# Two-layer mixer, projection and mixture-of-experts kernel: the first batch's mixers in two halves of the tokens

## The chip, the cores and the metric

The kernel runs on one core of a Trainium2 chip. The metric is the device time of one execution, in microseconds; times given here are the median of three executions, or one profiled execution where a profile is read. PE is TensorE (matrix multiply), DVE is VectorE, ACT is ScalarE, POOL is GpSimd, SP is SyncE, which here only issues transfers. ACT and POOL issue transfers too, from the same in-order instruction queue as their other work.

## The reference, cut to what matters

Four batches of 1024 tokens with 1024 channels each. Layer 0 mixes the tokens and projects; layer 1 mixes them with other constants and goes through a routed mixture of experts with a shared expert.

```
def mixer(r, k, w, u, cond):              # k is also v; time t runs over 1024 tokens, per channel
    tf    = sigmoid(sum(cond))            # one number per batch
    decay = exp(-exp(w)) * (0.5 + 0.5 * tf)
    ek, ekv = exp(min(k, 30)), exp(min(k, 30)) * k
    forward  sums:  a_t = a_(t-1) * decay + x_t      for x in (ek, ekv)
    backward sums:  the same from the last token to the first
    euk = exp(min(u + k, 30))
    num = forward(ekv) + backward(ekv) - ekv + euk * k
    den = forward(ek)  + backward(ek)  - ek  + euk
    return sigmoid(r) * num / max(den, 1e-8) * (0.8 + 0.2 * tf)

x = x + mixer(x, f, w0, u0, cond) @ (weight * scale).T + bias          # layer 0
h = mixer(x, f, w1, u1, cond)                                          # layer 1
x = x + h' + routed_experts(rmsnorm(h')) + shared_expert(rmsnorm(h'))  # h' = what the gate makes of h
```

The backward sum needs the tokens after a given one, the forward sum those before it. Both layers take the same `f` for k and v; sigmoid(r) of layer 1 depends on layer 0's result, so the kernel applies it later ("the gate").

## The kernel before, in words

**Mixers.** Channels lie on the 128 partitions, tokens on the free axis. A *unit* is one batch, one tile of 128 channels (`ct`, eight of them) and one layer (`L`), so there are 16 units per batch. For batch 0 all eight layer-0 units come first, then the eight of layer 1, each with its own load of k; for later batches the two layers of one `ct` follow each other and share k, `ek` and `ekv`. `mixing()` is a generator that runs a software pipeline: its iteration s does, in this order,

- "forth": the two forward scans of unit s (L281, DVE) into `fg`, and on ACT their scaling (L284) and the start values `tail` of the backward scans (L282);
- "back": `euk` of unit s-1 (L291, ACT) and its two backward scans in place (L293, DVE);
- "begin": min and exp of the next unit's k (L253 on DVE, L254 on ACT), where the next unit has a k of its own;
- "quotient" of unit s-2: four DVE passes in layer 0 (L311 to L315), three in layer 1 (L317);
- "times": `ekv` of the next unit (L259);
- "sums" of unit s-1: two DVE passes (L324, L325), a transfer from POOL that adds `euk` to `num` (L326), and the reciprocal on ACT by Relu, Ln, Exp (L329 to L331);
- transfers from ACT's queue: x for the sigmoid (L335, layer 0), the next k (L248), and the store of unit s-2's result to `c0_d` or `c1_d` (L341). Only then is unit s-2 in `made`.

ACT has one function table at a time: `exp_ln` and `other` keep track of it, and a sigmoid between exponentials costs a table load each way.

**Matrix work.** A chunk `q` is 512 tokens, so a batch has two. `first_ffn(q)` is layer 0's projection (eight *pieces* of 16 matmuls, L433), `late_gate(q)` the gate of chunks whose layer-1 mixer was not ready at that time, `norm_route(q)` norm and routing, `shared_up(q)` and `shared_down(q)` the shared expert (L645, L673). The experts follow in a last stage that this change does not touch.

**Order.** Every engine's instructions are in the order in which the program emits them. `order()` writes the order of pieces out by hand; `run` emits mixer steps ahead of each piece as long as `work["vector"] < pace[0] * work["tensor"]`, two sums of estimated costs (`W_SCANS` and the like, 6.9 for a piece). `pace` is 1.0 at first and 0.9 from the first `shared_up` on. `mix_until(units)` emits, at once, whatever steps are missing until the named units are `made`:

```
410  def early(ot):
...
416      if ot == 0:
417          mix_until(*((b, ct, 0) for ct in range(NC)))
...
422              nc.sync.dma_start(out=c0s[ct], in_=c0_d[b, ct, :, cols])
```

`early` of a piece is called two pieces ahead. So a `first_ffn` waits for all eight layer-0 units of its batch, and what is emitted after that call stands behind those steps in each queue. In batches after the first, the eighth layer-0 unit is the fifteenth of sixteen units.

Of the kernel before, what the change touches and what calls it, by code (L numbers as in the profile page):

```python
# [8 lines left out]
FP = mybir.dt.float32  # L9
I32 = mybir.dt.int32  # L10
U32 = mybir.dt.uint32
AF = mybir.ActivationFunctionType
ALU = mybir.AluOpType
# [9 lines left out]
P = 128  # L23
# [8 lines left out]
def kernel(  # L32
# [176 lines left out]

    W_SCANS, W_MIN, W_PASS, W_HALF = 4.7, 0.7, 1.25, 0.75  # L210
    W_PIECE, W_SMALL = 6.9, 1.0
    LATENCY = 12.0
    PACE = 0.9
    table = [None]

    def exp_ln(to, of, func, **kw):
# [5 lines left out]
    def other(to, of, func, **kw):  # L222
        table[0] = func
        nc.scalar.activation(to, of, func, **kw)

    units = [(0, ct, L) for L in range(2) for ct in range(NC)]
    units += [(b, ct, L) for b in range(1, B) for ct in range(NC) for L in range(2)]
    group = []  # L230
    for s, (b, ct, L) in enumerate(units):
        group.append(group[-1] if b > 0 and L == 1 else s - sum(1 for u in units[:s] if u[0] > 0 and u[2] == 1))
    made = set()

    def mixing():


        n = len(units)
        firsts = {}
        for s in range(n):  # L240
            firsts.setdefault(group[s], s)
        ks, of = {}, {}

        def fetch(g):
            if g in firsts:
                b, ct, _ = units[firsts[g]]
                ks[g] = pk.tile([P, T], FP, name="k")
                nc.scalar.dma_start(out=ks[g], in_=fT[b, bass.ts(ct, P), :])  # L248

        def begin(g):  # L250

            ek = p1.tile([P, T], FP, name="ek")
            nc.vector.tensor_scalar(ek, ks[g], 30.0, None, ALU.min)  # L253
            exp_ln(ek, ek, AF.Exp)  # L254
            return ek

        def times(ek, g):
            ekv = p1.tile([P, T], FP, name="ekv")
            nc.vector.tensor_tensor(ekv, ek, ks[g], ALU.mult)  # L259
            return ekv  # L260

        fetch(0)
        fetch(1)
        ek = begin(0)
        ekv = times(ek, 0)
        xg = None
        for s in range(n + 2):
            new, last, old = ((u if 0 <= u < n else None) for u in (s, s - 1, s - 2))
            if old is not None and units[old][2] == 0:
                other(xg, xg, AF.Sigmoid)  # L270
            if new is not None:

                b, ct, L = units[new]
                dk = decay[L][:, ct, b : b + 1]
                fg = pfg.tile([P, 2, T], FP, name="fg")
                tail = pfg.tile([P, 2], FP, name="tail")
                of[new] = fg, tail
                for m, x in enumerate((ek, ekv)):  # L280
                    nc.vector.tensor_tensor_scan(fg[:, m, :], dk.to_broadcast([P, T]), x, 0.0, ALU.mult, ALU.add)  # L281
                nc.scalar.activation(tail, fg[:, :, T - 1], AF.Copy, scale=dk)  # L282
                flat = fg.rearrange("p a t -> p (a t)")
                nc.scalar.activation(flat, flat, AF.Copy, scale=rest[L][:, ct, b : b + 1])  # L284
                yield W_SCANS
            if last is not None:
                b, ct, L = units[last]
                fg, tail = of[last]

                euk = p1.tile([P, T], FP, name="euk")  # L290
                exp_ln(euk, ks[group[last]], AF.Exp, bias=v[f"u{L}"][:, ct : ct + 1])  # L291
                for m in range(2):
                    nc.vector.tensor_tensor_scan(  # L293
                        fg[:, m, ::-1],
                        decay[L][:, ct, b : b + 1].to_broadcast([P, T]),
                        fg[:, m, ::-1],
                        tail[:, m : m + 1],
                        ALU.mult,
                        ALU.add,
                    )  # L300
                yield W_SCANS
            begun = s + 1 < n and group[s + 1] != group[s]
            if begun:
                ek = begin(group[s + 1])
                yield W_MIN
            if old is not None:
                b, ct, L = units[old]
                den, num = of[old][0][:, 0, :], of[old][0][:, 1, :]

                done = r  # L310
                nc.vector.scalar_tensor_tensor(den, den, 1e-8, r, ALU.max, ALU.mult)  # L311
                nc.vector.scalar_tensor_tensor(done, den, 2.0, r, ALU.subtract, ALU.mult)
                if L == 0:
                    nc.vector.scalar_tensor_tensor(done, done, nosc[:, b : b + 1], num, ALU.mult, ALU.mult)
                    nc.vector.tensor_tensor(done, done, xg, ALU.mult)  # L315
                else:
                    nc.vector.tensor_tensor(done, done, num, ALU.mult)  # L317
                yield W_PASS * (4 - L)
            if begun:
                ekv = times(ek, group[s + 1])  # L320
                yield W_PASS
            if last is not None:
                den, num = of[last][0][:, 0, :], of[last][0][:, 1, :]
                nc.vector.scalar_tensor_tensor(den, euk, E30, den, ALU.min, ALU.add)  # L324
                nc.vector.scalar_tensor_tensor(euk, euk, E30, ks[group[last]], ALU.min, ALU.mult)  # L325
                nc.gpsimd.dma_start(out=num, in_=euk, accum_op=ALU.add)  # L326

                r = p2.tile([P, T], FP, name="r")
                nc.scalar.activation(r, den, AF.Relu, bias=ntiny)  # L329
                exp_ln(r, r, AF.Ln, bias=tiny)  # L330
                exp_ln(r, r, AF.Exp, scale=-1.0)  # L331
                if units[last][2] == 0:
                    b, ct, _ = units[last]
                    xg = pxg.tile([P, T], FP, name="xg")
                    nc.scalar.dma_start(out=xg, in_=xT[b, bass.ts(ct, P), :])  # L335
                yield 2 * W_PASS
            if begun:
                fetch(group[s + 1] + 1)
            if old is not None:
                b, ct, L = units[old]  # L340
                nc.scalar.dma_start(out=(c0_d, c1_d)[L][b, ct], in_=done)  # L341
                of.pop(old)
                made.add(units[old])

# [59 lines left out]
    def first_ffn(q, gated):  # L404
# [4 lines left out]
        def early(ot):  # L409
            if not gated:  # L410

                nc.sync.dma_start(out=resT_d[ot, :, bass.ts(q, CH)], in_=xT[b, bass.ts(ot, P), cols])
            else:
                xs[ot] = px.tile([P, CH], FP, name="x")
                nc.sync.dma_start(out=xs[ot], in_=xT[b, bass.ts(ot, P), cols])
            if ot == 0:
                mix_until(*((b, ct, 0) for ct in range(NC)))
                if q == 0:
                    work["tensor"] += LATENCY
                for ct in range(NC):  # L420
                    c0s.append(pc0.tile([P, CH], FP, name="c0"))
                    nc.sync.dma_start(out=c0s[ct], in_=c0_d[b, ct, :, cols])
            tiles[ot] = pw0.tile([P, NC, P], FP, name="w0t")
            nc.sync.dma_start(out=tiles[ot], in_=w0[ot])
            if gated:
                mix_until((b, ot, 1))
                c1s[q, ot] = (ph, pc1)[q % NCH].tile([P, CH], FP, name="c1")
                nc.sync.dma_start(out=c1s[q, ot], in_=c1_d[b, ot, :, cols])

# [20 lines left out]
    def gate(q, ot, x, lag=1):  # L450
# [7 lines left out]
            other(held["y"], x, AF.Sigmoid, bias=v["b0"][:, ot : ot + 1])  # L458


        each = q == 0
        if ot == 0:
            accs[q] = pacc.tile([P, CH], FP, name="acc")
        square = accs[q] if ot == 0 and not each else None
# [29 lines left out]
    def late_gate(q):  # L494
# [3 lines left out]
        xs = {}  # L498

        def load(ot):  # L500
            mix_until((b, ot, 1))
            c1s[q, ot] = (ph, pc1)[q % NCH].tile([P, CH], FP, name="c1")
            nc.sync.dma_start(out=c1s[q, ot], in_=c1_d[b, ot, :, cols])
            xs[ot] = px.tile([P, CH], FP, name="x")
            nc.sync.dma_start(out=xs[ot], in_=resT_d[ot, :, bass.ts(q, CH)])
# [388 lines left out]

    def order():

        pieces = first_ffn(0, False) + first_ffn(1, False) + late_gate(0)

        pieces.insert(-1, Piece(lambda: None, tensor=LATENCY / 3))
        pieces += [Piece(lambda: None, tensor=0.5) for _ in range(7)]  # L900

        def slower():
            pace[0] = PACE
            work["tensor"] = max(work["tensor"], work["vector"] / PACE)

        pieces.append(Piece(slower, tensor=0.0))
        up, gates = shared_up(0), late_gate(1)
        for i, piece in enumerate(up):
            pieces.append(piece)
            if i % 2 == 1:  # L910
                pieces.append(gates.pop(0))
        pieces += gates
        pieces += shared_down(0) + shared_up(1) + shared_down(1)
        pieces += first_ffn(2, True) + first_ffn(3, True) + shared_up(2) + shared_down(2) + shared_up(3)
        for b in range(2, B):
            q = NCH * b
            pieces += first_ffn(q, True) + first_ffn(q + 1, True) + shared_down(q - 1)
# [476 lines left out]
```

## Time and profile before

| what | value |
|---|---|
| median of three executions | 5108.35 us (5101.46 to 5109.7) |
| profiled execution | 5109.81 us, span 5107.8 us |
| busy: PE, DVE, ACT, POOL | 94%, 61%, 28%, 16% of the span |
| first matmul of `first_ffn(0)` | 197.09 us |
| first matmul of `shared_up(0)` | 370.61 us |
| first matmul of `first_ffn(2)` | 728.57 us |
| one forward scan of 1024 tokens | 2.28 us |
| one table load on ACT | 1.283 us |

Times count from the start of the span. The stages that matter are four: the layer-0 mixers of batch 0 with PE idle, the first two projections, the gate and routing of the first chunk with PE mostly idle, and from `shared_up(0)` to `first_ffn(2)` a stretch in which PE is busy and DVE works off batch 1's mixers. After `first_ffn(2)` the same pattern repeats by batch with a full PE.

### The profile page before, as it was taken

The numbers are of one execution on the slowest core, as the hardware profiler recorded it, in microseconds if no ns is written. First come the engines' busy times: TensorE is split into PE (matmuls) and PEld (weight loads), VectorE is DVE, ScalarE is ACT, GpSimd is POOL, SyncE is SP. The second block draws the span as 40 slices with busy tenths as digits, with TensorE's granted clock in tenths as the row PEclk, the third lists the DMA queues.
The fourth block names the chain that finished last, engine by engine and source line by source line (L and its number), as shares of the span: only waits on it lengthen the run. The fifth ranks groups of instructions, "written<-read, shape, count | busy, mean of one in ns | idle before, by whom it ended". The sixth has DMA issues, their size and how long they took to land.

```text
span 5107.8 us, 36503 instructions
## 1 busy us (share of the span) xinstructions
PE 4823.9 (94%) x12906; PEld 2235.0 (44%) x12906; DVE 3130.7 (61%) x3280; ACT 1445.5 (28%) x1840; POOL 818.4 (16%) x765
## 2 busy tenths in 40 slices
PE   0479999999999998999999999999999999999999
PEld 0124444444444443444444444444444444444444
DVE  9988887887860222656565656556565656565621
ACT  5557656566540210111111111111111111111110
POOL 0113202302310220111111111111111111111110
PEclk9989999999999999999999999999999999999999
DMA  4678679669754845676767676767676777777784
GB/s 139 192 206 216 181 222 269 174 198 277 194 160 127 236 128 189 214 233 220 233 216 241 212 241 212 241 214 239 214 239 214 239 229 224 229 224 229 224 233 118
DMA packets 524212, 1077.77 MB, mean 211 GB/s; under 512 B 30642, under 2 KB 260147, under 8 KB 523411
## 3 DMA queue, kind: packets, MB, share of 16 engines
q1 hardware_dynamic: 386338, 744.70, 42.9%
q0 software_dynamic: 74656, 223.12, 20.9%
q10 hardware_dynamic: 63024, 107.50, 6.0%
q8 instruction: 105, 1.72, 0.1%
q14 instruction: 89, 0.72, 0.0%
HBM read 844.13 MB, written 203.56 MB: 205 GB/s over the span
## 4 chain that ended last, share of the span: by engine, by line
PE 60%; ACT 0%; issue 0%; DVE 0%; ACTq 0%
PE gA L1117 14%; PE gC L1117 9%; PE gB L1117 9%; PE dA L1117 7%; PE dB L1117 5%; PE dC L1117 5%; PE tr L971 2%; PE gA L1005 2%; PE gB L1005 2%; PE tr L1054 1%; PE dA L1067 1%; PE dB L1067 1%; PE gB L1305 0%; PE gC L1305 0%; PE gA L1305 0%; PE dA L1305 0%
## 5 line engine op out<-in xcount | busy, mean ns | idle before, releaser
L645 PE MATMUL mm<-c,wpc 128*128 128x512 f32 x1792 | 777.7, 593 | 0.9 <-DMA wpc<-in_su 0.9
L433 PE MATMUL mm<-c,w0t 128*128 128x512 f32 x1024 | 447.9, 599 | 213.9 <-DMA w0t<-in_w 212.4
L645 PEld LDWEIGHTS mm<-c,wpc 128*128 128x128 f32 x1792 | 337.9, 190 | 416.1 <-issue 412.5
L1117 PE MATMUL gA<-w,hsT 128*128 128x512 f32 x1088 | 489.6, 593 | 0.0
L1117 PE MATMUL gC<-w,s_up 128*128 128x512 f32 x1088 | 489.1, 592 | 0.0
L1117 PE MATMUL gB<-t_up,s_up 128*128 128x512 f32 x1088 | 489.1, 592 | 0.0
L1101 POOL DMA_INDIRECT sum_d<-y,tokens x148 | 306.3, 2070 | 917.2 <-DMA sum_d<-y,tokens 541.8
L871 POOL DMA_INDIRECT hs<-h_d,tokens x146 | 147.7, 1012 | 1621.8 <-PE tr L971 1540.3
L433 PEld LDWEIGHTS mm<-c,w0t 128*128 128x128 f32 x1024 | 196.2, 192 | 461.8 <-issue 456.4
L673 PE MATMUL mm<-sact,wpc 128*128 128x512 f32 x896 | 395.2, 596 | 0.0
L1117 PEld LDWEIGHTS gB<-t_up,s_up 128*128 128x128 f32 x1088 | 206.7, 190 | 260.2 <-issue 244.2
L1117 PEld LDWEIGHTS gC<-w,s_up 128*128 128x128 f32 x1088 | 206.7, 190 | 260.2 <-issue 260.2
L838 DVE TENSOR_TENSOR t_up<-w,w 128x2048 f32<-128x2048 f32 x136 | 310.7, 2285 | 0.0
L1117 PEld LDWEIGHTS gA<-w,hsT 128*128 128x128 f32 x1088 | 201.7, 190 | 227.8 <-issue 227.8
L293 DVE TENSOR_TENSOR_SCAN fg<-decay,tail,fg 128x1024 f32<-128x1024 f32 x128 | 292.9, 2330 | 0.0
L1117 PE MATMUL dB<-t_down,s_down 128*128 128x512 f32 x544 | 256.9, 595 | 0.1
L1117 PE MATMUL dA<-w,actT 128*128 128x512 f32 x544 | 255.8, 592 | 0.0
L1117 PE MATMUL dC<-w,s_down 128*128 128x512 f32 x544 | 255.8, 592 | 0.0
L972 ACT COPY hsT<-tr 128x512 f32<-128x512 f32 x296 | 172.7, 588 | 291.8 <-PE tr L971 291.8
L673 PEld LDWEIGHTS mm<-sact,wpc 128*128 128x128 f32 x896 | 168.1, 191 | 198.2 <-issue 196.7
L1117 PE MATMUL gA<-t_up,hsT 128*128 128x512 f32 x544 | 244.5, 592 | 0.0
L1042 ACT ACTIVATE act<-c 128x512 f32<-128x512 f32 x68 | 42.8, 630 | 708.9 <-DVE c L1038 708.9
(245 smaller groups left out, 6210.8 us busy)
## 6 DMA issues: line engine op xcount, KB each, us to landing
w<-in_w SPq DMA_DIRECT2D x240, 2048.0 KB, 9.1
fg<-euk POOLq DMA_DIRECT2D x64, 512.0 KB, 6.5
c_d<-r ACTq DMA_DIRECT2D x64, 512.0 KB, 7.9
c<-c_d SPq DMA_DIRECT2D x128, 256.0 KB, 6.8
w0t<-in_w SPq DMA_DIRECT2D x64, 512.0 KB, 6.4
wpc<-in_sg SPq DMA_DIRECT2D x56, 512.0 KB, 5.0
wpc<-in_su SPq DMA_DIRECT2D x56, 512.0 KB, 5.0
wpc<-in_sd SPq DMA_DIRECT2D x56, 512.0 KB, 5.4
```

What stands on the lines that cost most here:

```text
L293: nc.vector.tensor_tensor_scan(fg[:, m, ::-1], decay[L][:, ct, b : b + 1].to_broadcast([P, T]), fg[:, m, ::-1], tail[:, m : m + 1], ALU.mu ...
L433: nc.tensor.matmul(mm, lhsT=tiles[ot][:, it, :], rhs=c0s[it], start=(it == 0), stop=(it == NC - 1))
L645: nc.tensor.matmul(mm, lhsT=wts[f, n][:, kt, :], rhs=c1s[q, kt], start=(kt == 0), stop=(kt == NC - 1))
L673: nc.tensor.matmul(mm, lhsT=wts[ct][:, f, :], rhs=acts[q, f], start=(f == 0), stop=(f == NSI - 1))
L838: nc.vector.tensor_tensor(to, x, y, ALU.subtract)
L871: nc.gpsimd.indirect_dma_start(out=to, out_offset=None, in_=h_d, in_offset=bass.IndirectOffsetOnAxis(ap=have["tokens"][:, i, n : n + 1], a ...
L971: nc.tensor.transpose(tr[:, r, :], hs[:, bass.ts(4 * q + r, P)], ident)
L972: nc.scalar.copy(self.hsT[:, 4 * q : 4 * q + 4, b, :], tr)
L1005: nc.tensor.matmul(ps, lhsT=self.hsT[:, k, 0, :], rhs=w[k // NK][:, k % NK, bass.ts(n, I)], start=(k == 0), stop=(k == NC - 1),)
L1067: nc.tensor.matmul(ps, lhsT=self.actT[:, k, 0, :], rhs=w[:, k, bass.ts(n, 512)], start=(k == 0), stop=(k == NI - 1),)
L1101: nc.gpsimd.indirect_dma_start(out=sum_d, out_offset=bass.IndirectOffsetOnAxis(ap=tokens[:, i, self.n : self.n + 1], axis=0), in_=y, in_of ...
L1117: nc.tensor.matmul(ps, lhsT=x[:, k, :], rhs=w[:, k, :], start=(k == 0 and not more), stop=(k == half - 1), skip_group_check=more,)
```

## The change

Batch 0's units become half-units with a fourth field `part`: part 1 is the last 512 tokens, part 0 the first 512. All part-1 units of a layer come first, then all part-0 units. A part-1 unit runs both forward scans over all 1024 tokens, but back, quotient and sums for the last half only; it copies the backward scans' states to `carry` (two new DVE copies of one column), and ACT puts the scaled first halves of the forward scans into buffers that other stages own and that are idle then (`places`). A part-0 unit takes these, starts its backward scans from `carry`, and does the rest for the first half; its half of k is loaded again, and it runs sums ahead of the quotient (`early`). The load of x moves from the end of "sums" to the start of the next iteration for half-units. Chunk 1 is projected, gated and sent through the shared expert ahead of chunk 0 (`FIRST = 1`), and `late_gate(0)` runs beside `shared_up(1)`. `pace` becomes 0.97 up to the end of `first_ffn(2)` and 0.9 after that. Later batches keep their steps.

```diff
-    units = [(0, ct, L) for L in range(2) for ct in range(NC)]
-    units += [(b, ct, L) for b in range(1, B) for ct in range(NC) for L in range(2)]
+    units = [(0, ct, L, part) for L in range(2) for part in (1, 0) for ct in range(NC)]
+    units += [(b, ct, L, None) for b in range(1, B) for ct in range(NC) for L in range(2)]
...
+        def fetch_x(s):
+            b, ct, L, _ = units[s]
+            if L == 0:
+                xgs[s] = pxg.tile([P, T], FP, name="xg")[:, columns(s)]
+                nc.scalar.dma_start(out=xgs[s], in_=xT[b, bass.ts(ct, P), columns(s)])
+
+        def places(L, ct):
+            if L == 0:
+                return pa.tile([P, CH], FP, name="sact"), ph.tile([P, CH], FP, name="c1")
+            other_one = pr.tile([P, CH], FP, name="rT") if ct < 4 else pc0.tile([P, CH], FP, name="c0")
+            return ph.tile([P, CH], FP, name="c1"), other_one
...
+        def forth(s, x):
+            b, ct, L, part = units[s]
...
+            if part == 0:
+                of[s] = kept.pop((ct, L)), [carry[ct][:, m : m + 1] for m in range(2)]
+                return
...
+                nc.scalar.activation(fg[:, :, CH:T], fg[:, :, CH:T], AF.Copy, scale=scale)
+                kept[ct, L] = places(L, ct)
+                for m, to in enumerate(kept[ct, L]):
+                    nc.scalar.activation(to, fg[:, m, 0:CH], AF.Copy, scale=scale)
...
+        def back(s):
...
+            euk = p1.tile([P, T], FP, name="ekv" if part == 0 and ct % 2 == 0 else "euk")[:, columns(s)]
...
+                if part == 1:
+                    nc.vector.tensor_copy(carry[ct][:, m : m + 1], fg[m][:, 0:1])
...
             if old is not None and units[old][2] == 0:
-                other(xg, xg, AF.Sigmoid)
+                other(xgs[old], xgs[old], AF.Sigmoid)
+            if last is not None and units[last][3] is not None:
+                fetch_x(last)
             if new is not None:
...
+                forth(new, (ek, ekv))
+                if units[new][3] != 0:
+                    yield W_SCANS
             if last is not None:
...
+                euk = back(last)
+                yield W_SCANS * share(last)
             begun = s + 1 < n and group[s + 1] != group[s]
-            if begun:
+            fresh = begun and units[s + 1][3] != 0
+            early = last is not None and units[last][3] == 0
+            if fresh:
                 ek = begin(group[s + 1])
                 yield W_MIN
+            if early:
+                add_sums(last, euk)
+                yield 2 * W_PASS * share(last)
             if old is not None:
...
+                quotient(old)
+                yield W_PASS * (4 - units[old][2]) * share(old)
...
-                mix_until(*((b, ct, 0) for ct in range(NC)))
-                if q == 0:
+                mix_until(*(unit_of(q, ct, 0) for ct in range(NC)))
+                if q == FIRST:
                     work["tensor"] += LATENCY
...
-        pieces = first_ffn(0, False) + first_ffn(1, False) + late_gate(0)
+        pieces = first_ffn(FIRST, False) + first_ffn(0, False) + late_gate(FIRST)
...
-        up, gates = shared_up(0), late_gate(1)
+        up, gates = shared_up(FIRST), late_gate(0)
...
-        pieces += shared_down(0) + shared_up(1) + shared_down(1)
-        pieces += first_ffn(2, True) + first_ffn(3, True) + shared_up(2) + shared_down(2) + shared_up(3)
+        pieces += shared_down(FIRST) + shared_up(0) + shared_down(0)
+        pieces += first_ffn(2, True) + slower(PACE[1]) + first_ffn(3, True) + shared_up(2) + shared_down(2) + shared_up(3)
```

## Prediction

> **What bounds the kernel now.** I read the 40 slices of the page first, then a table of stretches, then PE's timeline for the places where it stands still.
>
> ```profile
> PE   0479999999999998999999999999999999999999
> DVE  9988887887860222656565656556565656565621
> ```
>
> PE is full from the fourth slice on, so the whole loss lies in the first three; DVE is nearly full exactly there. The table of stretches (length, then PE, PEld, DVE, ACT, POOL busy, PE clock, DMA share, GB/s) says how near to full:
>
> ```profile
> 16.10:197.10 181.00, 0.01 (x1) 0.04 (x1) 174.70 (x119) 108.14 (x96) 7.97 (x9) 1.00 0.43 127
> 197.10:311.00 113.90, 111.99 (x256) 49.08 (x256) 110.19 (x72) 60.76 (x62) 19.23 (x22) 1.00 0.92 263
> 311.00:370.60 59.60, 26.46 (x45) 7.16 (x45) 39.55 (x40) 36.59 (x41) 9.58 (x11) 0.63 0.69 161
> 370.60:690.10 319.50, 315.09 (x805) 143.25 (x804) 270.14 (x247) 208.55 (x209) 76.02 (x92) 0.99 0.72 189
> ```
>
> DVE idles 6.3, 3.7, 20.0 and 49.4 us: 79 us of the 674 until 690.1, where it has made the last layer-0 unit of batch 1. PE's timeline:
>
> ```profile
> 197.09 56.85 PE L433 MATMUL mm<-c,w0t 128*128 128x512 f32 x128 [197.09 <-DMA w0t<-in_w]
> ...
> 370.61 7.03 PE L645 MATMUL mm<-c,wpc 128*128 128x512 f32 x16
> ...
> 728.57 7.03 PE L433 MATMUL mm<-c,w0t 128*128 128x512 f32 x16
> ```
>
> PE waits 197 us for eight mixers and most of 60 us for the gate and routing of one chunk; from 370.61 to `first_ffn(2)` at 728.57 it is full (358 us). What `first_ffn(2)` needs is stored late:
>
> ```profile
> 700.58 0.52 ACTq L341 DMA_DIRECT2D c_d<-r  x1
> ```
>
> From such a store to the first matmul takes 11 us (the one at 186.10, matmul at 197.09: store landing, reload, weights). So at `first_ffn(2)` DVE is only 728.6 - 711.6 = 17 us ahead of PE. That margin decides: an earlier PE is worth nothing beyond it unless DVE is earlier too. The forecast is a sum over DVE's queue.
>
> **Removed, added, moved.** *DVE, more work.* Nothing is removed. For batch 0 every pass of quotient and sums is cut in two. In the groups by line:
>
> ```profile
> L467 DVE SCALAR_TENSOR_TENSOR c<-c,nosc,y 128x512 f32<-128x512 f32 x15 | 11.2, 746 | 18.0 <-ACT y L224 14.8 <-issue 3.3
> L311 DVE SCALAR_TENSOR_TENSOR fg<-fg,r 128x1024 f32<-128x1024 f32 x23 | 28.0, 1217 | 0.0
> ```
>
> Two halves cost 1.49 us against 1.22: +0.27. With six such passes in layer 0 and five in layer 1, 8 x 11 x 0.27 = 24 us. A scan of 32 elements took 0.22 us and one of 1024 took 2.28, so 0.15 us is fixed: 32 more scan instructions, 5 us. 32 one-column copies at 0.14 us (the row of a one-element cast) plus the wait for the scan just ahead, 0.2 each, 6 us. That is 35; passes that nobody waits for follow each other 0.08 us early, so I take 32 us. The Trainium skill, VectorE: DVE Perf Modes, section on the TRN2 errata, speaks more kindly: a fixed term measured at about 150 cycles, amortized from 512 elements on. At 0.156 us for 88 passes, 32 scans and 32 copies that would be 24 us. The rows are of these very shapes; I keep 32.
>
> *DVE, work moved.* At 370.6 DVE had done 36 us of batch 1: three pairs of forward scans (13), two of backward scans (9), sums, begin and times (9), a quotient (5). With half-units, about 3.4 of layer 1's eight first halves (6 us each: backward scans 2.4, sums 1.4, three passes 2.2) are still open when `shared_up` starts, 20 us. So 56 us of DVE work go behind PE's restart.
>
> *ACT's loop, a new wait.* In layer 0 the part-0 steps are short: DVE needs 2.4 (back) + 1.4 (sums) + 3.1 (quotient) = 6.9 us. But `early` puts the quotient last, and the store of its result stands at the end of ACT's queue for that iteration, ahead of the next sigmoid and the next `euk`. The rows of ACT:
>
> ```profile
> 121.32 2.00 ACT L284 ACTIVATE fg<-fg,rest 128x2048 f32<-128x2048 f32 x1
> 123.34 1.28 ACT L219 ACT_TABLE_LOAD   x1
> 124.63 1.15 ACT L220 ACTIVATE euk<-k,v_u 128x1024 f32<-128x1024 f32 x1
> ```
>
> After the quotient: issue of the store 0.45, table load 1.28, sigmoid of 512 elements 0.6, table load 1.28, `euk` 0.65 = 4.3 us, with DVE's backward scans beside it for 2.4. DVE idles 1.9 us in each of six iterations, 12 us, and about 6 us more in the iterations on both sides of this stretch (`euk` behind the reciprocal of the last part-1 unit; the sum into `num`, 5.4 to 6.8 us to land in the quiet stage, no longer covered by two forward scans). A rule of the skill speaks harder against the change: ScalarE: Activation LUTs, What ACT_TABLE_LOAD costs, puts a switch at 1283 ns plus a drain of 1380. That would make the loop 7.1 us and the idle 28 instead of 12. The trace shows 1283 and the next activation 0.01 us after it, so 12.
>
> *Other ACT work*: scaling in three instructions instead of one (1.06 + 2 x 0.59 against 2.0), halves of Relu, Ln, Exp and `euk`; at most 2 us per unit, covered by 13 us of DVE in a part-1 iteration.
>
> *Transfers.* In batch 0, k is issued 32 times instead of 16, stores 32 instead of 16, x 16 instead of 8: 40 more issues at 0.4 us on ACT's queue, covered except for the store in the loop. POOL issues 16 more sums at 0.87 us, covered while POOL is 8% to 20% busy. k's load is issued 6.5 us before "begin" instead of 7.6, because the back step between is shorter; k lands in 3.4 / 7.0 / 9.4 us (least, median, most), in a burst now shorter by half. DVE waited 3.7 us for k before; I take 7, between 2 and 15. x is issued an iteration earlier, which removes ACT's 3.7 us waits for it; these held nobody up. The loads for `late_gate(0)` pass SP's queue ahead of shared-expert weights, but by my count of the emitted steps the units they need are two gates ahead; zero, up to 5 us if not. The idle buffers: each is released before its owner wants it, zero.
>
> *Order and pace.* I summed the planner's own costs through `run`. Before, the last layer-0 unit of batch 1 is emitted five pieces ahead of `first_ffn(2)`, nothing forced. After, even at 0.97, 30 us of steps are forced two pieces ahead of it. PE then stands still until DVE is through.
>
> *Idle time of DVE until batch 1's last layer-0 unit*: start 6 (as before), loop and its edges 18, k 7, gate and routing stretch 22 (20 before), then 24 instead of 49, because 0.97 and the backlog leave fewer gaps (waits for PE, 17, vanish; waits for routing and ACT stay). Sum 77, against 79.
>
> **The sum.** That unit is through at 690 + 32 - 2 = 720 instead of 690. Its store follows about 4 us later (sums, then Relu, Ln, Exp; before, ACT was held up and took 10), the matmul 11 us after that: 735. PE's own path: first matmul at about 146 (16 + a first 21 us + 6 x 13.4 + 19 for the last handovers + 10), `first_ffn(0)` not before 230, `shared_up` at 370.6 - 56 + 28 (the part of the 32 that falls there) + 24 (idle added before it) = 366, `first_ffn(2)` no sooner than 366 + 358 = 724. DVE is later, so 735 against 728.6: +6.5 us. After it, both kernels are at the same step of batch 2 with the pace at 0.9, so this difference is carried to the end. Against the profiled execution, 5109.8 + 6.5 = 5116.3; that one is 1.5 us above the median of three, so 5115.
>
> **Rivals.**
> - *DVE fills its gaps* (faster). If the stretch after the restart leaves DVE only 10 us idle and the ACT loop costs 6, DVE is through 20 us sooner; PE's `shared_up` starts at about 355 and `first_ffn(2)` at 713 to 715: 5094. For it: 270 of 319 us busy there before, with 17 us of pure waiting for PE. Against it: DVE's queue is in order, and routing makes it wait 9 us in one piece.
> - *Sums into `num` queue behind the routing's scatters* (slower). From 388 to 416 POOL issued 16 scatters, 1.47 us each, and was busy 9 of 10 us. After the change, layer 1's first halves run there, with a sum every 6 us instead of 16.6 and only about 6.6 us from its issue to its use. If sums land later than that (256 KB sums took 7.6 to 10.3 us in that stretch), each of up to eight quotients waits about 2.5 us, DVE loses 20 us, and `first_ffn(2)` starts at 755: 5135. It decides once landing passes 6.6 us for most of them. I put 2 us of it into the 24 above.
> - *It does nothing*: the planner still holds PE until 190. The emitted steps exclude nearly all of it.
>
> **How the numbers follow.** The forecast gets 0.55 (alone 5102 to 5128), the faster rival 0.20, the slower 0.23, no effect 0.02. About 0.2%, 10 us, is what a measurement of this kernel can tell from no change. Faster by more: 0.18 of the first rival + 0.02 = 0.20. Slower by more: 0.23 + a third of the forecast, 0.19 = 0.42. Within: 0.38. The range, 5092 to 5142, cuts the fast end of the first rival and the far end of the second.
>
> **What would show it.** First matmul at 140 to 155; a PE gap of 20 to 35 us between the first two projections; in layer 0's first halves a step about every 8.8 us with DVE idle 1.9 for `euk`; `shared_up` at 355 to 375; a PE gap of about 10 us ahead of `first_ffn(2)`. I am wrong if half passes take under 0.65 us, if `shared_up` starts before 350 or if `first_ffn(2)` follows it by 358 us with no gap.

## The result and the profile after

The changed kernel takes 5168.9 us (median of 4 runs, 5166.9 to 5171.5) against 5105.6 us for the kernel before in the same comparison: 1.0124 times as long, with a 95% interval of 1.0107 to 1.0142. It is slower by 63 us, far outside the forecast range. The profiled execution has a span of 5165.1 us against 5107.8 (that one, of the kernel before, was 4 us above the median, this one 2 us below), so 57.3 us are there to be found.

The two rows of the page that carried the bound, now of the changed kernel:

```profile
PE   0668989999999999999999999999999999999999
DVE  8777999797780221665665656565656566565621
```

PE is busy in more of the second slice (6 instead of 4), as the change intends. The loss shows in the DVE row: its first four slices, 9 9 8 8 before, are 8 7 7 7.

The table of stretches of the changed kernel (start:end, length, then busy PE, PEld, DVE, ACT, POOL with counts, PE clock, DMA share, GB/s). The cuts are the first matmul, the start of `shared_up`, and the end of DVE's work on batch 1's last layer-0 unit:

```profile
16.10:140.50 124.40, 0.00 (x0) 0.00 (x0) 110.25 (x124) 87.16 (x108) 8.69 (x10) 1.00 0.45 128
140.50:367.20 226.70, 143.18 (x300) 57.86 (x301) 174.18 (x202) 139.45 (x182) 36.20 (x42) 0.80 0.75 196
367.20:761.20 394.00, 361.40 (x908) 162.90 (x906) 334.22 (x307) 246.07 (x250) 76.20 (x98) 0.96 0.68 184
```

DVE idles 14.2, 52.5 and 59.8 us: 126.5 us in all, against 79 before. Its busy time up to the same unit is 618.7 us against 594.6, 24.1 us more; and there are 155 more instructions, 152 of which are the added ones.

PE's timeline of the changed kernel (start, length, instructions, in brackets the idle time ahead and its releaser):

```profile
140.54 43.81 PE L495 MATMUL mm<-c,w0t 128*128 128x512 f32 x96 [140.54 <-DMA w0t<-in_w]
...
236.28 57.46 PE L495 MATMUL mm<-c,w0t 128*128 128x512 f32 x128 [23.97 <-DMA w0t<-in_w]
...
367.24 7.03 PE L707 MATMUL mm<-c,wpc 128*128 128x512 f32 x16
...
514.28 16.38 PE L735 MATMUL mm<-sact,wpc 128*128 128x512 f32 x34 [9.27 <-DVE sact L716]
...
768.80 1.08 PE L740 MATMUL tr<-ident,rT 128*128 128x128 f32 x4 [13.62 <-DVE rT L749]
775.21 9.60 PE L495 MATMUL mm<-c,w0t 128*128 128x512 f32 x16 [5.32 <-DMA w0t<-in_w]
```

PE starts 57 us sooner, but `shared_up` only 3.4 us sooner, and from there to `first_ffn(2)` it takes 408 us instead of 358, with waits on the way (9.27) and just ahead of it (13.62 and 5.32). In these stretches PE stands still for 45.5 us against 4.4, and it is busy 362.5 us against 353.6 with the same matmuls (913 and 912 in the traces). The starts of the later pieces say where the rest goes; in the last row, how far the changed kernel is behind:

| | `shared_up` | `first_ffn(2)` | `first_ffn(4)` | `first_ffn(6)` | span |
|---|---|---|---|---|---|
| before | 370.6 | 728.6 | 1150.3 | 1633.1 | 5107.8 |
| after | 367.2 | 775.2 | 1201.1 | 1690.9 | 5165.1 |
| behind by | -3.4 | 46.6 | 50.8 | 57.8 | 57.3 |

So 50 us are lost between `shared_up` and `first_ffn(2)`, 11 us between `first_ffn(2)` and `first_ffn(6)`, and nothing after that. Such starts are read from one execution each: run 14 below is the same program up to `first_ffn(2)` and has it at 779.4, so they spread by a few us.

What DVE waited for between `shared_up` and `first_ffn(2)`: first the kernel before (370.6 to 690.1), then the changed kernel (367.2 to 761.2). The columns are the waiting engine, tile and line, the releaser, total us, times, and the longest:

```profile
DVE sact L654 <- PE mm L645: 17.4, 5, 13.0
DVE lg L556 <- PE small L553: 9.3, 1, 9.3
DVE c L467 <- ACT y L224: 5.8, 4, 3.9
DVE sact L654 <- ACT sact L224: 5.3, 1, 5.3
DVE fg L324 <- ACT euk L220: 3.5, 1, 3.5
```

```profile
DVE c L529 <- ACT y L225: 14.1, 4, 6.0
DVE sact L716 <- PE mm L707: 10.3, 1, 10.3
DVE c L352 <- ACT euk L221: 8.4, 2, 4.9
DVE ekv L276 <- DMA c<-ekv: 7.0, 1, 7.0
DVE ek L270 <- DMA k<-in_fT: 6.7, 1, 6.7
```

These are the longest of each. Summed over the whole lists, waits for PE fall from 28 us to 10, waits for ACT rise from 18 to 32, and 14 us of waits for transfers (a load of k, and a buffer that a transfer still reads) are new. The last two stand side by side. DVE, then POOL, then ACT's queue of the changed kernel:

```profile
395.54 2.45 DVE L325 TENSOR_TENSOR_SCAN c<-decay,carry,c 128x512 f32<-128x512 f32 x2
404.67 0.69 DVE L270 TENSOR_SCALAR ek<-k 128x1024 f32<-128x1024 f32 x1 [6.68 <-DMA k<-in_fT]
...
415.76 1.23 DVE L276 TENSOR_TENSOR ekv<-ek,k 128x1024 f32<-128x1024 f32 x1 [7.01 <-DMA c<-ekv]
```

```profile
407.25 0.94 POOL L354 DMA_DIRECT2D c<-ekv  x1 [3.19 <-issue]
```

```profile
394.67 0.59 ACT L609 COPY hr<-tr 128x512 f32<-128x512 f32 x1 [0.45 <-ACT hr L609]
395.29 0.33 ACTq L610 DMA_DIRECT2D h_d<-hr  x1
395.65 0.52 ACTq L265 DMA_DIRECT2D k<-in_fT  x1
```

`hr` is routing's copy, `c<-ekv` the adding transfer of a first half, `h_d<-hr` and `k<-in_fT` issues on ACT's queue. The load of k is issued at 395.65, behind routing's copies on ACT, and is used at 404.67, 9 us later; the steps between issue and use hold only 2.5 us of DVE work. Then `ekv` cannot be written: a first half has used that buffer for its `euk`, and the adding transfer that reads it is issued at 407.25, among the scatters, and frees the buffer at about 415.7. In those 20 us (395.5 to 415.8) DVE waits 13.7 us.

### The profile page after: what moved, and what is told of

The parts are those of the page before. It is cut to its first block, busy times and chain, and to the rows that moved or that the text cites. A ratio compares the mean times of both kernels' runs of the same rounds, so it can differ in the third digit from the quotient of the medians.

```text
span 5165.1 us, 36964 instructions
## 1 busy us (share of the span) xinstructions
PE 4844.4 (94%) x12906; PEld 2241.6 (43%) x12906; DVE 3151.5 (61%) x3432; ACT 1504.7 (29%) x1972; POOL 821.5 (16%) x781
## 4 chain that ended last, share of the span: by engine, by line
PE 59%; ACT 0%; issue 0%; DVE 0%; ACTq 0%
PE gA L1182 14%; PE gC L1182 9%; PE gB L1182 9%; PE dA L1182 7%; PE dB L1182 5%; PE dC L1182 5%; PE tr L1036 2%; PE gA L1070 2%; PE gB L1070 2%; PE tr L1119 1%; PE dA L1132 1%; PE dB L1132 1%; PE dA L1370 0%; PE gC L1370 0%; PE gA L1370 0%; PE gB L1370 0%
## 5 line engine op out<-in xcount | busy, mean ns | idle before, releaser
L325 DVE TENSOR_TENSOR_SCAN fg<-decay,tail,fg 128x1024 f32<-128x1024 f32 (+1 forms) x128 | 260.2, 2064 | 0.0
```

Of the source, the lines that this page charges most:

```text
L325: nc.vector.tensor_tensor_scan(fg[m][:, ::-1], decay[L][:, ct, b : b + 1].to_broadcast([P, width]), fg[m][:, ::-1], init[m], ALU.mult, ALU ...
```

## The experiments

The ratios are to the kernel before, with 95% intervals; differences in us are between medians. Where a run is set against the changed kernel, run 5 or run 10, the intervals can overlap, but all executions of the one were faster than all of the other.

**1. Sums on DVE.**

```diff
-            nc.gpsimd.dma_start(out=num, in_=euk, accum_op=ALU.add)
+            if units[s][2] == 1 and units[s][3] == 0:
+                nc.vector.tensor_tensor(num, num, euk, ALU.add)
+            else:
+                nc.gpsimd.dma_start(out=num, in_=euk, accum_op=ALU.add)
```

> The changed kernel, but the sums into num of layer 1's first halves are made by DVE (8 instructions of about 0.7 us) instead of an adding transfer of POOL. Theory A (DVE idles because half steps are shorter than the queues they go through: POOL's scatters, ACT's tables and stores): the 9 us that ekv L276 waits for the transfer out of its buffer go, and some of the wait for k behind them; DVE does 5.5 us more; with the PE gaps that follow, 5155 to 5163. Theory B (the pace of 0.97 is what costs): 5170 to 5175, the added work and nothing back. Theory C (only the work that was moved and added counts, idle time is made up somewhere): 5174.

Measured: 5160.3 us, 1.0106 (1.0090 to 1.0123), 9 us less than the changed kernel. The 7.0 us for `ekv` are gone and the wait for k fell from 6.7 to 2.9, as Theory A said; `first_ffn(2)` starts at 764.4 instead of 775.2, although the eight sums are 5.5 us more work for DVE (0.69 us each).

**2. Stores behind the next exponential.**

```diff
-                nc.scalar.dma_start(out=(c0_d, c1_d)[L][b, ct, :, columns(old)], in_=rs.pop(old))
-                of.pop(old)
-                made.add(units[old])
+                if units[old][3] == 0 and s < n and units[s][3] == 0:
+                    waiting.append(old)
+                else:
+                    store(old)
...
                 euk = back(last)
+                while waiting:
+                    store(waiting.pop())
```

> The changed kernel, but in the first halves the store of a quotient is issued on ACT's queue after the next unit's exponential, instead of before it (two units share one r tile so that it stays alive). Theory A: the 1.9 us idle per first-half step of layer 0 (16 us of waits of sact for ACT in the trace) is mostly gone, shared_up starts 8 to 14 us sooner than 367, and the total falls to about 5157. Theory B: shared_up sooner by as much, but first_ffn(2) unmoved, 5169. Theory C: the same as B.

Measured: 5154.6 us, 1.0096 (1.0079 to 1.0113), 14 us less. In its profiled execution `shared_up` starts at 350.8 (16 us sooner) and `first_ffn(2)` at 752.0 (23 us sooner), but that execution took 5145.0 us, 10 us less than the other three; by the medians about as much arrives at the end as was gained at `shared_up`. In the changed kernel the loop looks as the prediction drew it (DVE's wait, then ACT's queue between two of them):

```profile
164.64 0.69 DVE L352 SCALAR_TENSOR_TENSOR sact<-ekv,sact 128x512 f32<-128x512 f32 x1 [2.02 <-ACT ekv L221]
...
173.29 0.69 DVE L352 SCALAR_TENSOR_TENSOR sact<-euk,sact 128x512 f32<-128x512 f32 x1 [2.02 <-ACT euk L221]
```

```profile
168.93 0.33 ACTq L403 DMA_DIRECT2D c_d<-r  x1
169.29 1.28 ACT L225 ACT_TABLE_LOAD   x1 [1.21 <-DVE r L346]
...
171.24 1.28 ACT L220 ACT_TABLE_LOAD   x1
172.53 0.72 ACT L221 ACTIVATE euk<-k,v_u 128x512 f32<-128x512 f32 x1
```

A step takes 8.65 us (164.64 to 173.29) and DVE waits 2.02 us in it: 8.8 and 1.9 were predicted. In the last step the wait is 8.52 us instead, since ACT stood 7.76 us; that one is absent from this run, and was not foreseen. Up to 200 us DVE waits 23.0 us for these exponentials in the changed kernel and 9.6 us in this run, so the move of the store is the cause of most of it; what held ACT in the last step was not taken apart.

**3. The pace back to 0.90.**

```diff
-    PACE = 0.97, 0.9
+    PACE = 0.9, 0.9
```

> The changed kernel with the planner's pace at 0.90 instead of 0.97 in the stretch after the restart. Theory B: PE's waits between 400 and 590 us (about 26 us) go, since fewer mixer steps stand ahead of its evictions, and the total falls by 15 to 30 us, to 5140-5155. Theory A: more steps are forced ahead of first_ffn(2) (about 58 us instead of 30), PE's early waits are exchanged for a longer one there: 5169 to 5185. Theory C: 5169.

Measured: 5177.7 us, 1.0139 (1.0122 to 1.0156), 9 us more. `first_ffn(2)` starts at 784.4, behind a longer stand of PE than the 13.62 us of the changed kernel:

```profile
778.01 1.08 PE L740 MATMUL tr<-ident,rT 128*128 128x128 f32 x4 [37.71 <-DVE rT L749]
```

In the changed kernel, then, the pace of 0.97 is worth 9 us; Theory B falls as a cause of the whole loss.

**4. Halves in layer 1 only.**

```diff
-    units = [(0, ct, L, part) for L in range(2) for part in (1, 0) for ct in range(NC)]
+    units = [(0, ct, 0, None) for ct in range(NC)] + [(0, ct, 1, part) for part in (1, 0) for ct in range(NC)]
```

> The changed kernel with batch 0's layer 0 whole, as before the change, and only layer 1 in halves. Half of the added DVE work (12 us) and ACT's loop of layer 0's first halves go; PE starts at about 197 again. Theory A: idle of DVE up to 367 falls by some 15-20 us, shared_up starts at about 350, the stretch after it keeps its idle time of 55-60: first_ffn(2) at about 745, total 5135 to 5145. Theory B: the pace still costs, first_ffn(2) follows shared_up by 400 us: also shared_up at 350, total 5150. Theory C: only the 12 us of work go: 5157.

Measured: 5153.0 us, 1.0090 (1.0073 to 1.0107). No theory had this right: `shared_up` starts at 396.8, later than in both kernels. The two stretches of DVE up to that point:

```profile
16.00:195.70 179.70, 0.00 (x0) 0.03 (x1) 171.51 (x126) 107.50 (x103) 7.81 (x9) 1.00 0.44 127
195.70:396.80 201.10, 140.18 (x300) 57.21 (x301) 151.79 (x168) 102.51 (x139) 34.08 (x40) 0.83 0.79 205
```

DVE is busy 323 us in them, as long as up to `shared_up` in the kernel before (324): all eight first halves of layer 1 stand ahead of the gate that PE waits for, so nothing is gained. The delay of 26 us is idle time, 57 us against 30, again in waits for k, for `euk` and for sums. DVE is through with the layer-0 unit early enough (store at 741, `first_ffn(2)` at 761.2), so here PE is the bound.

**5. Both edits, 1 and 2, together.** The diffs are those above.

> The changed kernel with both of the edits before: sums of layer 1's first halves on DVE, and stores issued after the next exponential. Theory A (half steps are shorter than the queues of POOL and ACT that they go through): the two gains add up, 9 + 14 us below 5169, 5144 to 5149; the rest, 38 to 43 us over the kernel before, is then added DVE work and waits of DVE that have no POOL or store in them. Rival (both take away the same waiting time): 5152 to 5156.

Measured: 5146.1 us, 1.0077 (1.0061 to 1.0092), 23 us less: the gains add up. `first_ffn(2)` starts at 750.7, 24.5 us sooner than in the changed kernel (run 12, the same program up to there, has 750.7 too). DVE still idles 47.1 us after `shared_up`:

```profile
353.20:737.00 383.80, 357.91 (x908) 161.84 (x906) 336.74 (x311) 245.84 (x250) 75.16 (x94) 0.97 0.67 186
```

**6. Swap and pace without halves.** The kernel before, with only these parts of the change:

```diff
+    FIRST = 1
-    PACE = 0.9
+    PACE = 0.97, 0.9
...
-        pieces = first_ffn(0, False) + first_ffn(1, False) + late_gate(0)
+        pieces = first_ffn(FIRST, False) + first_ffn(0, False) + late_gate(FIRST)
...
-        pieces += first_ffn(2, True) + first_ffn(3, True) + shared_up(2) + shared_down(2) + shared_up(3)
+        pieces += first_ffn(2, True) + slower(PACE[1]) + first_ffn(3, True) + shared_up(2) + shared_down(2) + shared_up(3)
```

> The kernel before with only the rest of the change: the first two chunks change places and the pace is 0.97 up to first_ffn(2); no halves. If the halves are the cause (theory A), nothing much moves: within 6 us of the kernel before, since PE is full from shared_up to first_ffn(2) and DVE is 17 us ahead there. If the swap or the pace costs on its own (theory B), 15 us or more are lost here: 5120 to 5140.

Measured: 5130.6 us, 1.0046 (1.0031 to 1.0061), 23 us more than before. Against Theory A's forecast: part of the loss needs no halves. Runs 9 and 10 take it apart.

**7. The cuts alone.**

```diff
+                for h in parts(b):
-                nc.vector.scalar_tensor_tensor(den, den, 1e-8, r, ALU.max, ALU.mult)
+                    nc.vector.scalar_tensor_tensor(den[:, h], den[:, h], 1e-8, r[:, h], ALU.max, ALU.mult)
```

and so on for every backward scan, sum and quotient of batch 0; `parts` gives both halves for batch 0 and the whole for the others.

> The kernel before with batch 0's backward scans, sums and quotients cut into two instructions each (88 more passes, 32 more scans, 32 column copies), in the same order and the same steps, nothing moved. This is the added DVE work alone, 24 us by the trace of the changed kernel. DVE bounds everything up to shared_up, so shared_up starts about 24 us later than 370.6 (some of it in gaps: 18 to 24) and the total is 5125 to 5131. If the 17 us by which DVE is ahead at first_ffn(2) absorb it: 5107 to 5115.

Measured: 5126.8 us, 1.0038 (1.0024 to 1.0051), 19 us more. `shared_up` starts at 392.3 (21.7 later) and `first_ffn(2)` at 754.1 (25.5 later); PE's stretch between them is 362 us. After that nothing is lost. (This execution was 7 us above the median, so the starts are late by up to that.) DVE up to `shared_up`:

```profile
16.00:213.70 197.70, 0.00 (x0) 0.03 (x1) 188.94 (x211) 108.03 (x96) 7.96 (x9) 1.00 0.43 117
213.70:392.30 178.60, 137.55 (x300) 56.20 (x301) 158.75 (x171) 96.66 (x102) 28.75 (x33) 0.86 0.83 221
```

It is busy 23 us longer than before (347.7 against 324.4), which is the added work by itself, and `shared_up` is 22 us later: added DVE work ahead of it comes through one for one. The 17 us by which DVE is ahead at `first_ffn(2)` do not help, since PE itself starts late.

**8. The gate first.** The kernel before, with the planner told to emit no mixer step of its own accord between the start of `late_gate(0)` and `shared_up(0)`:

```diff
-            while work["vector"] < pace[0] * work["tensor"] and mix():
+            while not held[0] and work["vector"] < pace[0] * work["tensor"] and mix():
```

> The kernel before, with no batch-1 mixer steps emitted between the start of late_gate(0) and shared_up(0) beyond those that the last layer-1 unit needs (about 18 us of DVE work moved behind shared_up). This tests the margin of 17 us by itself. If PE's start is what sets first_ffn(2) there and DVE has 17 us in hand: shared_up 8 to 12 us sooner, 5095 to 5100. If moved DVE work always comes back at first_ffn(2) (the change's failure in small): 5104 to 5112.

Measured: 5143.6 us, 1.0071 (1.0057 to 1.0085), 36 us more, outside both forecasts. `shared_up` starts at 367.2, only 3.4 us sooner, though DVE is busy 11.5 us less up to it: the chain of gate, norm and routing waits for its own stages. The store of the unit falls from 700.6 to 722.8, so the 17 us are spent, and `first_ffn(2)` is 7.6 us late. The larger part, 30 us, is lost after it. PE's timeline there, in this run:

```profile
1327.11 1.12 PE L546 MATMUL tr<-ident,c 128*128 128x128 f32 x4 [9.31 <-ACT rT L680]
1400.11 1.12 PE L546 MATMUL tr<-ident,c 128*128 128x128 f32 x4 [7.94 <-ACT rT L680]
```

Together they are 17.3 us; in the kernel before no such wait reaches 0.3 us there. L680 is ACT's copy of a result of the shared expert; it frees the buffer that routing's transposes need. At 1326.49 it stands in ACT's queue behind a mixer step, a sigmoid that itself waited 3.46 us for x and a scaling of 2.00 us. The two waits are more than half of the 30 us; the rest is not taken apart.

**9 and 10. Swap alone, pace alone**, in the kernel before. Run 9 is run 6 with this edit; run 10 has the lines of run 6 that set the pace, and not those of the swap.

```diff
-    PACE = 0.97, 0.9
+    PACE = 0.9, 0.9
```

> The kernel before with only the first two chunks swapped (pace 0.90 as before, no halves). Swap plus pace cost 23 us together. If the swap is the cause, 5125 to 5132 here; if the pace is, within 5 us of the kernel before, 5103 to 5113.

Measured: 5111.4 us, 1.0007 (1.0001 to 1.0014), 4 us. The swap is nearly free. Run 9 also sets the planner's count anew after `first_ffn(2)`, as `slower` does there, so that is not what costs.

> The kernel before with only the pace at 0.97 up to first_ffn(2) (no swap, no halves). If the pace is the cause of the 23 us: 5125 to 5132, with PE's waits in batch 2 (after first_ffn(2)) longer by some 15 us, as in the run with both. If the swap is the cause: 5103 to 5113.

Measured: 5133.8 us, 1.0057 (1.0040 to 1.0073), 27 us more. The pace is the cause of the 23 us of run 6. Its stretch from `shared_up` to the end of batch 1's last layer-0 unit, and PE's timeline:

```profile
373.20:672.50 299.30, 289.87 (x743) 131.59 (x742) 267.46 (x242) 202.53 (x205) 76.45 (x92) 0.98 0.73 192
```

```profile
501.72 17.23 PE L673 MATMUL mm<-sact,wpc 128*128 128x512 f32 x34 [8.35 <-DVE sact L654]
...
805.26 37.08 PE L433 MATMUL mm<-c,w0t 128*128 128x512 f32 x80 [11.85 <-DVE c L467]
```

With whole units the pace does what the prediction relied on: DVE idles 31.8 us instead of 49.4, and the unit is done 18 us sooner. But PE then waits for evictions that stand behind mixer steps on DVE (8.35 us), `first_ffn(2)` starts 9 us late (737.4), and 17 us more go between it and `first_ffn(6)`.

**11. Halves in layer 0 only.**

```diff
-    units = [(0, ct, L, part) for L in range(2) for part in (1, 0) for ct in range(NC)]
+    units = [(0, ct, 0, part) for part in (1, 0) for ct in range(NC)] + [(0, ct, 1, None) for ct in range(NC)]
```

> The changed kernel with halves in layer 0 only, layer 1 whole. Theory A: PE starts at 140; the waits of ACT's loop (16 us) and half of the added DVE work stay, so shared_up starts no sooner than 375 to 395 (all of layer 1 must be through before the first gates end); waits for POOL's sums and the ekv buffer after the restart go; first_ffn(2) at 745 to 760, total 5130 to 5150, with 10 to 20 us of it lost after first_ffn(2). If halves of layer 1 are harmless and layer 0's are the whole loss: 5165.

Measured: 5164.8 us, 1.0117 (1.0100 to 1.0134). PE starts at 140.5 and then waits 71.5 us for the gate's stages; `shared_up` starts at 403.3. That is 58 us of loss with half of the change, and run 4, the other half, has 46: the parts do not add up, so the loss can't be shared out between the layers. An earlier first matmul alone is worth nothing here.

**12 to 14. The steps of batch 2 back in their places.** The 11 us after `first_ffn(2)` were open. A credit on the planner's count is meant to put the mixer steps back at the pieces where they stand in the kernel before, by the planner's own costs; nothing else changes. Run 12 has both edits of run 5, run 14 is the changed kernel, and run 13 is run 10 with -34.0 in place of 4.4.

```diff
-        def slower(to):
+        def slower(to, ahead=0.0):
...
-                work["tensor"] = max(work["tensor"], work["vector"] / to)
+                work["tensor"] = max(work["tensor"], work["vector"] / to) + ahead
...
-        pieces += first_ffn(2, True) + slower(PACE[1]) + first_ffn(3, True)
+        pieces += first_ffn(2, True) + slower(PACE[1], 4.4) + first_ffn(3, True)
```

> The run with both fixes (5146), with 4.4 us of credit added to the planner's count of PE work after first_ffn(2). By the planner's own costs that puts the mixer steps from first_ffn(3) on at the same pieces as in the kernel before. In all runs in which they stand elsewhere, 11 to 30 us are lost between first_ffn(2) and first_ffn(6); where they stand as before, none. If the place of the steps is the cause, those 11 us go: 5133 to 5138, with first_ffn(2) unmoved at 751. If the loss comes from a DVE that is still behind, nothing moves: 5143 to 5149.

> The kernel before with the pace at 0.97 up to first_ffn(2) (5134), and 34 us taken off the planner's count after it, which puts the mixer steps of batch 2 from the end of first_ffn(3) on at the same pieces as in the kernel before. If the place of the steps is what the 0.97 cost after first_ffn(2) (17 us of its 26): 5113 to 5120. If the pace's cost comes from something else: 5130 to 5137.

> The changed kernel itself (5169), with the 4.4 us of credit alone. Place of the steps: 11 us less, 5155 to 5160, first_ffn(2) at 775 as in the changed kernel. If DVE being behind is the cause: 5166 to 5172.

Measured: 5134.5 us (1.0055, 1.0038 to 1.0072), 12 us less than run 5; 5124.4 us (1.0032, 1.0018 to 1.0047), 9 us less than run 10 and 4 us over the forecast's upper end; 5161.7 us (1.0106, 1.0089 to 1.0122), 7 us less than the changed kernel and 2 us over that end. From `first_ffn(4)` to `first_ffn(6)`, in the kernel before, the changed kernel, run 12, run 13:

```profile
1150.29:1633.10 482.81, 474.22 (x1206) 213.78 (x1205) 287.72 (x282) 218.02 (x229) 86.94 (x108) 0.99 0.67 192
```

```profile
1201.13:1690.94 489.81, 478.38 (x1206) 215.36 (x1204) 292.46 (x286) 220.17 (x231) 85.75 (x108) 0.99 0.66 189
```

```profile
1177.28:1659.84 482.56, 474.36 (x1205) 214.10 (x1204) 287.62 (x282) 217.99 (x229) 85.94 (x108) 0.99 0.68 192
```

```profile
1165.37:1647.46 482.09, 474.60 (x1206) 213.95 (x1204) 287.69 (x282) 217.99 (x229) 86.84 (x108) 0.99 0.67 192
```

With the steps in place this stretch is as long as before, to 0.8 us, in all three (run 14: 483.0), with as many instructions on DVE and ACT. So these 7 us are the place of the steps. The other 4 to 5 us, between `first_ffn(2)` and `first_ffn(4)`, stay in runs 12 and 14 (426.6 us against 421.7). In the changed kernel and in run 12 PE waits 7.1 and 7.4 us there for one load of weights (5.3 in the kernel before) and is busy 2.4 and 2.8 us longer; why the load comes later was not taken apart. Of the 17 us that run 13 still loses, 15 lie ahead of `first_ffn(4)`.

## Why the prediction was wrong, point by point

- **The start was right.** First matmul at 140.5 (146 predicted), a gap of 24 us between the first two projections (20 to 35), `first_ffn(0)` at 236 (not before 230), ACT's loop at 8.65 us per step (8.8). The Trainium skill's rule for a table switch (ScalarE: Activation LUTs, What ACT_TABLE_LOAD costs) would have made this step longer by a drain of 1380 ns at each switch, which the trace does not show (a load from 171.24 to 172.52, the next exponential at 172.53); trusting the row was right there. That DVE, and not PE, sets `first_ffn(2)` was right too.
- **`shared_up` at 367 (366 predicted) was right by luck: two errors cancel.** By the prediction's own terms DVE should have been busy 297 us from 16.1 us to that point and idle 53; it was busy 284 and idle 67. Nearly all of the 14 us more idle time lies in ACT's loop and at its edges: 31 us between 118 and 236 us instead of 18, with the last step's 8.52 us as the longest wait.
- **The term of added DVE work was too large:** 32 us, measured 24.1, and 23 in run 7, which has nothing else. Its passes were sized from the 0.746 row, which has a scalar operand from memory. The half passes of the changed kernel, by shape:

```profile
L343 DVE SCALAR_TENSOR_TENSOR r<-fg,r 128x512 f32<-128x512 f32 x16 | 11.1, 692 | 0.6
...
L342 DVE SCALAR_TENSOR_TENSOR fg<-fg,r 128x512 f32<-128x512 f32 x16 | 10.9, 684 | 0.0
...
L345 DVE SCALAR_TENSOR_TENSOR r<-r,nosc,fg 128x512 f32<-128x512 f32 x8 | 6.0, 752 | 1.6 <-DMA fg<-euk 1.4
```

  Only the one pass with `nosc`, a scalar from memory, costs 752 ns; the others cost 684 to 692, and two of them 0.15 to 0.16 us more than a whole pass (1217 to 1225). The prediction took the 0.746 row to be of the same kind, and it was not. Over 88 cuts that is 14 us, not 24. Here the estimate that the prediction made from the skill and set aside (VectorE: DVE Perf Modes, the TRN2 errata: a fixed term of about 150 cycles) was 24 us and agrees with the trace. This error alone would have made the forecast too slow, not too fast.
- **The step that failed: DVE's idle time, above all that after `shared_up`, "24 instead of 49".** It was 59.8. With the 14 us more ahead of `shared_up` and 8 us less work, this puts the unit at 761 instead of 720, and `first_ffn(2)` at 775 instead of 735. Two reasons stood behind the 24. One, that the pace of 0.97 and the backlog leave fewer gaps, holds for whole units (31.8 in run 10), but here 10 of the 17 us of waits for PE stay. The other, that waits for ACT and routing "stay" as they were, does not hold: with half units DVE waits for `euk` and `y` on ACT's queue, for k and for a shared buffer. (`y` alone: 14.1 us, against 5.6 in run 6, which has the swap and the same pace with whole units.) Runs 1, 2 and 5 show 24.5 us of such waits at `first_ffn(2)`, in both stretches together. No run removed the rest: in run 5 DVE still idles 47 us after `shared_up`, and there the cause is read from the trace alone (12.6 us for `y`, 8.0 for `euk`, 10.8 for PE).
- **The slower rival named the right queue and the wrong victim.** Sums do queue among POOL's scatters, but it is not eight quotients that wait: one whole unit waits for the buffer that a sum still reads. The prediction had put borrowed buffers at zero. Run 1 puts the sums of layer 1's first halves, buffer and all, at 9 us; the rival had 20.
- **"This difference is carried to the end" failed.** The pace is 0.9 in both kernels after `first_ffn(2)`, but the steps do not stand at the same pieces, and 11 us are lost there. Seven of them came back when the steps were put back.
- **A missing term: what 0.97 costs PE.** The prediction counted its gaps filled on DVE and no wait on PE. Run 10 shows 27 us for it alone, of which run 13 takes 9 back. In the changed kernel it still pays (run 3), since at 0.90 more steps are left to be forced ahead of `first_ffn(2)`, where PE stands still for them (37.71 us against 13.62).
- **None of the signs that the prediction named for being wrong came.** Half passes took more than 0.65 us, `shared_up` did not start before 350, and `first_ffn(2)` did not follow it by 358 us. A sign for the idle time itself was missing.

Put together for the profiled span: 24.5 us of waits that runs 1 and 2 remove, 22.1 us that are left of the delay at `first_ffn(2)` in run 5, and 11.2 us after it; 0.5 us come back later, which makes 57.3. The 22.1 us are not the added work alone, though run 7, which has nothing else, shows a delay of about that size. In run 5 DVE is through with the unit at 737.0, 47 us later than before: 29 us are busy time (5 of it sums) and 18 idle time; the 17 us of margin and a store that follows the unit sooner take this to 22. With all three mended (run 12) 27 us of loss remain, and none of the fourteen beats the kernel before. The parts are not strictly separate.

## What to carry to other kernels

Halving a step halves the work that covers a load, an adding transfer or a table switch. It did not halve their durations here (1.28 us for a table load as before; 8.5 us for an adding transfer of half the size, among scatters, against 5.4 to 6.8 from issue to landing for the whole in the quiet stage of the kernel before). For each queue in the loop, compare the shorter step with the longest trip through that queue before counting on fewer gaps. Do not assume idle time of an in-order engine away because there is more to do: ask for each wait in the list what would end it. And where an order is planned to the piece, treat a shift of the steps as a cost of its own, and test it by putting the steps back: 7 to 12 us came back here in three runs.

## What the hardware showed that was not expected

A short wait costs PE more than itself, and the granted clock goes with it. In the changed kernel, from the stand of 13.62 us on:

```profile
760.00:780.20 20.20, 6.08 (x10) 2.90 (x11) 19.13 (x15) 9.35 (x10) 0.85 (x1) 0.50 0.63 194
780.20:800.00 19.80, 19.80 (x53) 9.14 (x52) 19.56 (x16) 13.72 (x14) 0.86 (x1) 1.00 0.99 333
```

The clock is 0.50 up to 780.2 and 1.00 after that. The 16 matmuls that start at 775.21 take 9.60 us: 5.0 us at half and 4.6 at full clock, which make 7.1 us of full clock, and 7.03 is what 16 take otherwise. The four transposes at 768.80 take 1.08 us, and most others 0.60. From `shared_up` to `first_ffn(2)` as a whole the clock is 0.95 against 1.00 before, and PE is busy 8.9 us longer; in the stretch with the most waits (140.5 to 367.2) it is 0.80. So part of what looks like more PE work is the waits once more.

The adding transfer of 256 KB held its source for about 8.5 us after its issue, and the load of k took 9 us from issue to use in the same stretch: both longer than the 6 us of DVE work in a half step of layer 1 behind which they were to hide.
